# Seven products instead of eight on two blocks of every second channel, with block sums on GpSimd and VectorE

## The chip, the cores and the metric

The kernel runs on one core of a Trainium2 chip. Five engines matter here, each with its own instruction queue that it works through in order: TensorE (PE; its weight loads are shown as PEld), VectorE (DVE), ScalarE (ACT), GpSimd (POOL) and SyncE (SP), which here only issues transfers. TensorE writes its results to PSUM, eight banks of 512 float32 numbers per partition[...]. Everything else lies in SBUF, 128 partitions wide. All numbers are float32.

The metric is the device time of one execution in microseconds, lower being better. The kernel before took 3156.9 us (median of three runs, 3156.66 to 3157.14).

## The reference

Two layers follow each other on an input x of 384 x 384 positions with 128 channels. The first is a gated triangle product:

```python
z = layernorm(x)
left  = (z @ Wl + bl) * sigmoid(z @ Wlg + blg)
right = (z @ Wr + br) * sigmoid(z @ Wrg + brg)
core  = einsum('bikh,bjkh->bijh', left, right)      # 128 channels h, each 384 x 384 x 384
x1 = x + sigmoid(x @ Wg + bg) * (layernorm(core) @ Wout + bout)
```

The second is a row gate: x1 goes through a left, an equality, a right and a gate matrix, the right part is summed along each row, the product goes through an output matrix, and the result plus x1 is normalised. The change touches the line `core = einsum(...)` alone. For each of the 128 channels it is one matrix product of a 384 x 384 left half, transposed, with a 384 x 384 right half.

## The kernel before, in words

The kernel has three stages. The first (up to about 1000 us) normalises x, makes left and right, and stores them to memory as `lr_d`, ordered by channel; one corner of the data, the last two groups of 64 columns in the last of the three row blocks, stays in SBUF (`kept`). The second makes the core, channel by channel, and is the stage that is changed. The third (from about 1760 us) works row by row on the core, and ends with the output.

Every instruction is pinned behind the one that was written before it for the same engine (`seq`), so the order of each engine's queue is the order of the program text. Waits between engines are placed by the data: an instruction waits for what it reads, and for the readers of what it overwrites.

The core stage runs over h from 0 to 127. N is 384, P is 128, NB is 3. Per channel:

- Loading (`load_h`, L92): two transfers on SP bring left and right of channel h, interleaved element by element, into one of three buffers `lrh`. The transfer for channel h + 3 is written after the work on channel h, because it takes that channel's buffer.
- Filling (`fill`, L576 to L595): GpSimd copies the kept corner into place (`stay`, L584 to L587: four copies of 128 x 64, two into `lrh` for the left half and two into `rr` for the right half), and then pulls the right half out of the interleaved buffer into a contiguous one, `rr` (L592: two blocks, L593: the rest of the third). `rr` has two buffers. Channel h + 1 is filled while TensorE works on channel h.
- Multiplying (L610 to L614): nine products, row block by row block, each with a 128 x 128 block of the left half as weights and one 128 x 384 block of `rr` as moving operand. They accumulate in three PSUM banks, `pc`, of which there are two sets. A product of float32 is two instructions on TensorE.
- Draining (L620 to L627): ScalarE copies all three banks to `ct` (two buffers), then squares it into `sq` (one buffer). VectorE adds `ct` to the running sum `csum` (L622) and `sq` to the running sum of squares `csq` (L623). Both are 128 x 1152, and third-stage statistics come from them. SP stores `ct` to `core_d`, after the transfer for channel h + 3.

Channel 127 is treated apart: its first block is finished ahead, and the inverse deviation of that block is computed while the rest goes on (`variance`, `root`, `inverse`, `newton`, L527 to L559; buffers `ve`, `r` and `m` from a pool of their own).

Of the kernel before, what the change touches and what calls it, by code (L numbers as in the profile page):

```python
# [19 lines left out]
def triangle_then_gated_row_kernel(ctx: ExitStack, tc: tile.TileContext, a: dict, out: bass.AP):  # L20
# [31 lines left out]
    core_d = dpool.tile([N, H, N], F32, name="core_d")  # L52
# [3 lines left out]
    def seq(ins):  # L56

        return tc.keep_in_program_order(ins)
# [21 lines left out]
    with ExitStack() as ctx2:  # L80
# [16 lines left out]
        with tc.tile_pool(name="p1w", bufs=5, side="right") as wp, \  # L97
# [361 lines left out]
            for k, (n, q) in enumerate(steps):  # L459
# [54 lines left out]
                if k == len(steps) - 2 * G // 4 + 16:  # L514
                    assert not full
                    for h in range(2):
                        load_h(h)


        spool, rp = (end2.enter_context(tc.tile_pool(name=n, bufs=b, side="right", reuse_waits="tile"))  # L520
                     for n, b in (("stats", 1), ("rstd", 2)))
        roots = {}


# [1 line left out]

        def variance(b, s):  # L527
            if b not in roots:
                roots[b] = [rp.tile([P, N], F32, tag=n, name=n, bufs=c) for n, c in (("ve", NB), ("r", NB), ("m", 2))]
            ve, _, m = (w[:, s] for w in roots[b])  # L530
            if b > 0:
                seq(nc.scalar.activation(m, csum[:, b, s], AF.Square, scale=1.0 / H))
                seq(nc.scalar.activation(ve, csq[:, b, s], AF.Copy, scale=1.0 / H))
                seq(nc.gpsimd.tensor_tensor(ve, ve, m, ALU.subtract))
                seq(nc.gpsimd.tensor_scalar(ve, ve, 0.0, EPS, ALU.max, ALU.add))
                return
            seq(nc.vector.scalar_tensor_tensor(m, csum[:, b, s], 1.0 / (H * H), csum[:, b, s], ALU.mult, ALU.mult))
            seq(nc.vector.scalar_tensor_tensor(ve, csq[:, b, s], 1.0 / H, m, ALU.mult, ALU.subtract))
            seq(nc.vector.tensor_scalar(ve, ve, 0.0, EPS, ALU.max, ALU.add))

        def root(b, s=None):
            ve, r, _ = roots[b]
            seq(nc.scalar.activation(r, ve, AF.Sqrt))

        def inverse(b, s):
            _, r, m = (w[:, s] for w in roots[b])
            seq(nc.vector.reciprocal(m, r))  # L547

        def newton(b, s):
            ve, r, m = (w[:, s] for w in roots[b])  # L550
            if b > 0:
                seq(nc.scalar.activation(r, m, AF.Square))
                seq(nc.gpsimd.tensor_tensor(r, r, ve, ALU.mult))
                seq(nc.gpsimd.tensor_scalar(r, r, -0.5, 1.5, ALU.mult, ALU.add))
                seq(nc.gpsimd.tensor_tensor(r, r, m, ALU.mult))
                return
            seq(nc.vector.tensor_mul(r, m, m))
            seq(nc.vector.scalar_tensor_tensor(r, r, -0.5, ve, ALU.mult, ALU.mult))
            seq(nc.vector.scalar_tensor_tensor(r, r, 1.5, m, ALU.add, ALU.mult))  # L559

        with tc.tile_pool(name="p2r", bufs=2, side="right", reuse_waits="tile") as rrp, \
             tc.tile_pool(name="p2more", bufs=1, side="right", reuse_waits="tile") as more, \
             tc.tile_pool(name="p2out", bufs=2, side="right", reuse_waits="tile") as op, \
             tc.tile_pool(name="p2sq", bufs=1, side="right", reuse_waits="tile") as qp, \
             tc.tile_pool(name="p2ps", bufs=2, space=PSUM, reuse_waits="tile") as ps, \
             tc.tile_pool(name="p2one", bufs=1, space=PSUM, reuse_waits="tile") as ps1:
            csum = spool.tile([P, NB, N], F32, name="csum")
            csq = spool.tile([P, NB, N], F32, name="csq")
            seq(nc.vector.memset(csum, 0.0))
            seq(nc.vector.memset(csq, 0.0))  # L570

            inp.append(more)
            load_h(2)
            right = {}

            def fill(h):  # L576

                if h < H:
                    t = loaded2[h]
                    rr = right[h] = rrp.tile([P, NB, N], F32, tag="rr", name="rr")  # L580
                    i1 = G * (NG - KEEP)

                    def stay():
                        for (kb, ig), lrt in kept.items():  # L584
                            i = slice(ig * G, (ig + 1) * G)
                            seq(nc.gpsimd.tensor_copy(t[:, kb, i, 0], lrt[:, h, :, 0]))
                            seq(nc.gpsimd.tensor_copy(rr[:, kb, i], lrt[:, h, :, 1]))  # L587


                    if h > 0:  # L590
                        stay()
                    seq(nc.gpsimd.tensor_copy(rr[:, :NB - 1], t[:, :NB - 1, :, 1]))  # L592
                    seq(nc.gpsimd.tensor_copy(rr[:, NB - 1, :i1], t[:, NB - 1, :i1, 1]))  # L593
                    if h == 0:
                        stay()  # L595

            fill(0)
            for h in range(H):
                fill(h + 1)
                t, rr = loaded2.pop(h), right.pop(h)  # L600
                pc = ps.tile([P, NB, 512], F32, tag="pc", name="pc")
                banks = [pc[:, ib, :N] for ib in range(NB)]
                order = [(kb, ib) for kb in range(NB) for ib in range(NB)]
                if h == H - 1:


                    banks[0] = ps1.tile([P, 512], F32, name="pc0")[:, :N]
                    order.sort(key=lambda o: o[1] > 0)
                    seq(nc.scalar.activation(warm, mhalf[:, 0:1], AF.Sqrt, scale=-1.0))
                for kb, ib in order:  # L610
                    seq(nc.tensor.matmul(  # L611
                        banks[ib], lhsT=t[:, kb, ib * P:(ib + 1) * P, 0], rhs=rr[:, kb],
                        start=(kb == 0), stop=(kb == NB - 1),
                    ))  # L614

                ct = op.tile([P, NB, N], F32, tag="ct", name="ct")
                sq = qp.tile([P, NB, N], F32, tag="sq", name="sq")
                to = core_d[:, h, :].rearrange("(b p) j -> p b j", p=P)
                if h < H - 1:
                    seq(nc.scalar.copy(ct, pc[:, :, :N]))  # L620
                    seq(nc.scalar.activation(sq, ct, AF.Square))
                    seq(nc.vector.tensor_add(csum, csum, ct))  # L622
                    seq(nc.vector.tensor_add(csq, csq, sq))  # L623
                    load_h(h + 3)

                    queue = nc.sync if h < H - 3 else nc.scalar
                    seq(queue.dma_start(out=to, in_=ct))  # L627
                else:
                    seq(nc.scalar.copy(ct[:, 0], banks[0]))
                    seq(nc.scalar.activation(sq[:, 0], ct[:, 0], AF.Square))  # L630
                    seq(nc.scalar.dma_start(out=to[:16, 0], in_=ct[:16, 0]))
                    seq(nc.scalar.dma_start(out=to[16:, 0], in_=ct[16:, 0]))
                    seq(nc.vector.tensor_add(csum[:, 0], csum[:, 0], ct[:, 0]))
                    seq(nc.vector.tensor_add(csq[:, 0], csq[:, 0], sq[:, 0]))
                    seq(nc.scalar.copy(ct[:, 1:], pc[:, 1:, :N]))  # L635
                    variance(0, slice(0, N))
                    root(0)
                    inverse(0, slice(0, N))
                    newton(0, slice(0, N))
                    seq(nc.scalar.dma_start(out=to[:, 1:], in_=ct[:, 1:]))  # L640


                    seq(nc.gpsimd.dma_start(out=rstd_d[0:P, :], in_=roots[0][1]))
                    seq(nc.gpsimd.tensor_tensor(sq[:, 1:], ct[:, 1:], ct[:, 1:], ALU.mult))
                    seq(nc.gpsimd.tensor_tensor(csum[:, 1:], csum[:, 1:], ct[:, 1:], ALU.add))
                    seq(nc.gpsimd.tensor_tensor(csq[:, 1:], csq[:, 1:], sq[:, 1:], ALU.add))

# [333 lines left out]
```

## Time and profile before

| What | Value |
|---|---|
| median of the runs | 3156.9 us |
| the profiled execution's own time | 3154.78 us |
| its span in the profile | 3152.9 us |
| TensorE busy | 3135.5 us (99%) |
| VectorE busy | 2473.6 us (78%) |
| GpSimd busy | 2392.9 us (76%) |
| ScalarE busy | 1808.5 us (57%) |
| core stage, 1100 to 1740 us: DMA share and rate | 0.96, 283 GB/s |
| granted TensorE clock | 0.999 of full |

The profile records one execution. A group line names the code line, the engine, the operation, what it writes and reads with shapes, how often it ran, its total busy time and mean duration, and, after the last bar, how long the engine was idle just before such instructions and what released it. A tile's line gives the least, the median and the largest duration. A timeline line gives the start, the duration, and then the instruction. Matmuls are pipelined: a matmul's own duration is longer than the distance between two of them, so distances are read from starts. A busy GpSimd or VectorE instruction may in part be waiting inside.

### The profile page before, as it was taken

The page shows a single profiled execution, that of the slowest core. Times are in us where ns is not written, and L with a number is a line of the kernel's source. Part 1 is how long each engine was busy: PE and PEld are TensorE (multiplying, and loading weights), DVE is VectorE, ACT ScalarE, POOL GpSimd, SP SyncE. Part 2 cuts the span into 40 slices and gives each one's busy share as a digit, 9 for nine tenths or more (in the row PEclk, how much of TensorE's full clock was granted, in tenths as well). Part 3 has the DMA queues.
Part 4 walks back from the last instruction along what each step waited for, and adds up shares of the span by engine and source line. Part 5 has one row for each costly group of instructions (what it writes and reads, how often), then busy time and mean ns, then how long its engine had stood idle before and what let it go on. Part 6 is the DMA issues. An engine that isn't in the chain of part 4 may idle for free.

```text
span 3152.9 us, 44536 instructions
## 1 busy us (share of the span) xinstructions
PE 3135.5 (99%) x11306; PEld 2132.8 (68%) x11306; DVE 2473.6 (78%) x7409; ACT 1808.5 (57%) x3755; POOL 2392.9 (76%) x3066
## 2 busy tenths in 40 slices
PE   9999999999999999999999999999999999999998
PEld 4777777777776666666666666677777777777776
DVE  8888888888885555555555788888888888888998
ACT  4444444444444343343433577777777777777777
POOL 6888888888886656666566587788888888888887
PEclk9999999999999999999999999999999999999999
DMA  4978878788883999999999865666666666666562
GB/s 154 340 302 304 326 279 340 281 320 299 312 304 106 282 282 283 282 284 282 284 282 283 298 231 202 220 224 221 219 220 218 221 220 219 220 220 222 210 213 109
DMA packets 509102, 797.42 MB, mean 253 GB/s; under 512 B 56689, under 2 KB 419569, under 8 KB 492466
## 3 DMA queue, kind: packets, MB, share of 16 engines
q1 hardware_dynamic: 507552, 792.61, 74.0%
q8 instruction: 94, 1.54, 0.2%
q10 hardware_dynamic: 1234, 1.77, 0.2%
q14 instruction: 158, 1.29, 0.1%
q0 software_dynamic: 64, 0.20, 0.0%
HBM read 508.14 MB, written 286.36 MB: 252 GB/s over the span
## 4 chain that ended last, share of the span: by engine, by line
PE 98%; DVE 1%; ACT 0%; issue 0%; DMA 0%; POOL 0%; POOLq 0%; DVEq 0%; ACTq 0%
PE pr L372 31%; PE pc L611 23%; PE py L781 8%; PE pr L752 8%; PE pg L769 8%; PE pl L770 8%; PE pg L721 8%; PE py L782 4%; DMA core_d<-ct 0%; PE pt L335 0%; PE pq L729 0%; ACT py L816 0%; PE pb L740 0%; POOL rs L286 0%; DVE m L547 0%
## 5 line engine op out<-in xcount | busy, mean ns | idle before, releaser
L372 PE MATMUL pr<-wz,xc 128*128 128x512 f32 x2176 | 935.1, 592 | 0.0
L372 PEld LDWEIGHTS pr<-wz,xc 128*128 128x128 f32 x2176 | 670.5, 308 | 263.9 <-POOL xc L324 1.2
L383 ACT ACTIVATE sg<-pr,rs 128x256 f32<-128x256 f32 x1152 | 483.8, 471 | 508.3 <-ACT sg L383 354.7
L611 PE MATMUL pc<-rr,lrh 128*128 128x384 f32 x2304 | 743.3, 486 | 0.4 <-DVE lr L385 0.4
L611 PEld LDWEIGHTS pc<-rr,lrh 128*128 128x128 f32 x2304 | 452.0, 196 | 291.8 <-issue 1.1
L385 DVE SCALAR_TENSOR_TENSOR lr<-pr,rs,sg 128x256 f32<-128x256 f32 x1152 | 501.7, 477 | 164.3 <-ACT sg L383 158.9
L816 ACT ACTIVATE py<-py,nm,rs 128x128 f32<-128x128 f32 x1149 | 493.1, 430 | 159.7 <-DVE u L774 80.6
L781 PEld LDWEIGHTS py<-wo,u 128*128 128x128 f32 x2304 | 376.6, 191 | 97.5
L622 DVE TENSOR_TENSOR csum<-csum,ct 128x1152 f32<-128x1152 f32 x127 | 175.0, 1378 | 332.9 <-ACT ct L620 332.9
L781 PE MATMUL py<-wo,u 128*128 128x128 f32 x2304 | 402.1, 275 | 0.0
L620 ACT COPY ct<-pc 128x1152 f32<-128x1152 f32 x127 | 142.3, 1120 | 445.2 <-PE pc L611 439.7
L743 POOL TENSOR_TENSOR cs<-ct,rt 128x384 f32<-128x384 f32 x380 | 379.7, 1000 | 8.3 <-DMA rt<-rstd_d 4.4
L851 POOL TENSOR_TENSOR yt<-yt,lnb 128x384 f32<-128x384 f32 x380 | 380.6, 1003 | 2.9 <-DVE yt L845 2.6
L324 POOL TENSOR_TENSOR xc<-xc,bc 128x512 f32<-128x512 f32 x272 | 345.8, 1271 | 24.0
L286 POOL TENSOR_TENSOR rs<-nd,mhalf 128x8 f32<-128x8 f32 (+1 forms) x145 | 236.3, 1630 | 146.8 <-ACT sg L383 107.2
L796 DVE BATCH_NORM_STATS2 st<-py 128x6 f32<-128x128 f32 x1152 | 266.0, 286 | 87.2 <-PE py L782 85.1
L592 POOL COPY rr<-lrh 128x768 f32<-128x768 f32 x128 | 190.8, 1490 | 167.2 <-DMA lrh<-lr_d 156.4
L782 PE MATMUL py<-ident,x1T 128*128 128x128 f32 x1152 | 314.0, 273 | 0.0
L752 PE MATMUL pr<-cs,wc 128*128 128x384 f32 x768 | 313.5, 490 | 0.0
L769 PE MATMUL pg<-x1T,mat_L_conv_W_gate 128*128 128x384 f32 x768 | 310.7, 486 | 0.9 <-ACT g L772 0.9
L721 PE MATMUL pg<-xt,mat_L_conv_Wg 128*128 128x384 f32 x768 | 310.7, 487 | 0.3 <-ACT ct L635 0.2
L770 PE MATMUL pl<-x1T,mat_L_conv_W_left 128*128 128x384 f32 x768 | 310.5, 486 | 0.0
(124 smaller groups left out, 4302.2 us busy)
## 6 DMA issues: line engine op xcount, KB each, us to landing
lr_d<-lr SPq DMA_DIRECT2D x128, 1024.0 KB
lrh<-lr_d SPq DMA_DIRECT2D x128, 640.0 KB
xt<-in_x_row_dram SPq DMA_DIRECT2D x96, 768.0 KB
ct<-core_d SPq DMA_DIRECT2D x95, 768.0 KB
rt<-rstd_d SPq DMA_DIRECT2D x95, 768.0 KB
out_dram<-yt SPq DMA_DIRECT2D x94, 768.0 KB
core_d<-ct SPq DMA_DIRECT2D x125, 576.0 KB
xt<-in_x_nat_dram SPq DMA_DIRECT2D x136, 512.0 KB
```

The costliest lines, as they stand in the source:

```text
L372: seq(nc.tensor.matmul(pr[:, r, :], lhsT=columns[n][:, 4 * q + i, :] if n < PLAIN else columns[n][:, q, :, i], rhs=wz, start=True, stop=Tr ...
L383: seq(nc.scalar.activation(sg[r], pr[:, r, 2 * H:], AF.Sigmoid, scale=rs[r]))
L385: seq(nc.vector.scalar_tensor_tensor(t[:, :, c * XR + r0 + r, :], pr[:, r, :2 * H].rearrange("k (h s) -> k h s", s=2), rs[r], sg[r].rearra ...
L611: seq(nc.tensor.matmul(banks[ib], lhsT=t[:, kb, ib * P:(ib + 1) * P, 0], rhs=rr[:, kb], start=(kb == 0), stop=(kb == NB - 1),))
L721: seq(nc.tensor.matmul(pg[:, :N], lhsT=wg0, rhs=r["xT"], start=True, stop=True))
L752: seq(nc.tensor.matmul(pr[:, :N], lhsT=wc, rhs=r["cs"], start=True, stop=True))
L769: seq(nc.tensor.matmul(pg2[:, :N], lhsT=wgate, rhs=r["x1T"], start=True, stop=True))
L770: seq(nc.tensor.matmul(pl[:, :N], lhsT=wleft, rhs=r["x1T"], start=True, stop=True))
L781: seq(nc.tensor.matmul(py[:, s], lhsT=r["u"][:, s], rhs=r["wo"], start=True, stop=False))
L782: seq(nc.tensor.matmul(py[:, s], lhsT=r["x1T"][:, s], rhs=ident, start=False, stop=True, is_transpose=True))
L816: seq(nc.scalar.activation(py[:, s], py[:, s], AF.Identity, bias=bias, scale=scale))
L851: seq(engine.tensor_tensor(yt, yt, lnbb, ALU.add))
```

## The change

Even channels are multiplied as before, nine full products (`plain`). Odd channels from 1 to 125 are multiplied differently. Take the left blocks as A(k, i), row block k and column block i, and cut each right block of 384 columns into two halves of 192, B(k, j). For k, i and j in {0, 1} the sum of A(k, i) times B(k, j) over k is a 2 x 2 product of blocks, which takes eight half-width products in the plain way. Strassen's identity, in the form with few additions, does it with seven, on sums of blocks:

- left sums on GpSimd (`left_sums`, four sums of 128 x 128, into `ss`)
- right sums on GpSimd (`right_sums2`, one instruction for two sums and two more of 192 columns, into `tt`)
- sums of the products on VectorE (`add`, eight sums of 192 columns with one operand from PSUM), and one copy by ScalarE (`one`).

The third row block of k adds four half products, which accumulate into the same banks, and the third column block i stays three full products into `b4`. So an odd channel is 11 half-width and 3 full products, 17 half-widths where there were 18.

Around that the change moves work. The right half of an odd channel is pulled out by ScalarE (`apart`, three copies), not by GpSimd; the kept corner is still copied by GpSimd, now in the even channel's part, ahead of the left sums. `pc` has one set of three banks, because the odd channels take the other five. The even channel's banks are copied by ScalarE early in the odd channel; its squares and its sum follow there, and its sum of squares is added in the next even channel. The odd channel's third block is copied by ScalarE in the next even channel, and so are its square and both sums. Both stores wait accordingly. `ct` has three buffers; the buffers for the sums, `sq` and the inverse deviations share one allocation (`arena`). The last two channels are multiplied and drained as before.

```diff
-        spool, rp = (end2.enter_context(tc.tile_pool(name=n, bufs=b, side="right", reuse_waits="tile"))
-                     for n, b in (("stats", 1), ("rstd", 2)))
+        spool = end2.enter_context(tc.tile_pool(name="stats", bufs=1, side="right", reuse_waits="tile"))
+        arena = spool.tile([P, 2 + 2 * NB, N], F32, name="arena")
+        own_root = [[arena[:, n] for n in place] for place in ((0, 1, 2), (3, 5, 7), (4, 6, 2))]
...
-                roots[b] = [rp.tile([P, N], F32, tag=n, name=n, bufs=c) for n, c in (("ve", NB), ("r", NB), ("m", 2))]
+                roots[b] = own_root[b]
...
-             tc.tile_pool(name="p2out", bufs=2, side="right", reuse_waits="tile") as op, \
-             tc.tile_pool(name="p2sq", bufs=1, side="right", reuse_waits="tile") as qp, \
-             tc.tile_pool(name="p2ps", bufs=2, space=PSUM, reuse_waits="tile") as ps, \
-             tc.tile_pool(name="p2one", bufs=1, space=PSUM, reuse_waits="tile") as ps1:
+             tc.tile_pool(name="p2out", bufs=3, side="right", reuse_waits="tile") as op, \
+             tc.tile_pool(name="p2st", bufs=1, side="right", reuse_waits="tile") as stp:
...
+            J = N // 2
+            js = slice(0, J), slice(J, N)
+            one, base, more2, least = (arena[:, n, j] for n in (2, 2 * NB) for j in js)
+            tt = arena[:, 0:2].rearrange("p b n -> p (b n)").rearrange("p (q j) -> p q j", j=J)
+            ss = [arena[:, 2 * NB + 1, n * P:(n + 1) * P] for n in range(3)] + [stp.tile([P, P], F32, name="s4")]
+            sq = arena[:, NB:2 * NB]
...
+            def block(h, k, i):
+                return loaded2[h][:, k, i * P:(i + 1) * P, 0]
...
+            def stay(h):
+
+                t, rr = loaded2[h], right[h]
+                for (kb, ig), lrt in kept.items():
+                    i = slice(ig * G, (ig + 1) * G)
+                    seq(nc.gpsimd.tensor_copy(t[:, kb, i, 0], lrt[:, h, :, 0]))
+                    seq(nc.gpsimd.tensor_copy(rr[:, kb, i], lrt[:, h, :, 1]))
+
+            def left_sums(h):
+
+                for n, x, y, op in ((0, block(h, 0, 1), block(h, 0, 0), ALU.subtract),
+                                    (1, block(h, 0, 1), block(h, 1, 1), ALU.add),
+                                    (2, ss[1], block(h, 0, 0), ALU.subtract),
+                                    (3, block(h, 1, 0), ss[2], ALU.subtract)):
+                    seq(nc.gpsimd.tensor_tensor(ss[n], x, y, op))
+
+            def right_sums2(h):
+
+                rr = right[h]
+                seq(nc.gpsimd.tensor_tensor(
+                    tt[:, 0:2], rr[:, 0, js[1]].unsqueeze(1).to_broadcast([P, 2, J]),
+                    rr.rearrange("p b n -> p (b n)").rearrange("p (a m) -> p a m", a=2)[:, :, js[0]], ALU.subtract,
+                ))
+                seq(nc.gpsimd.tensor_tensor(tt[:, 2], rr[:, 0, js[0]], tt[:, 1], ALU.subtract))
+                seq(nc.gpsimd.tensor_tensor(tt[:, 3], rr[:, 1, js[0]], tt[:, 2], ALU.subtract))
+
+            def apart(h, k):
+
+                j = slice(0, N if k < NB - 1 else G * (NG - KEEP))
+                seq(nc.scalar.copy(right[h][:, k, j], loaded2[h][:, k, j, 1]))
+
+            def squares(h):
+                seq(nc.scalar.activation(sq, cts[h], AF.Square))
+
+            def add_sum(h):
+                seq(nc.vector.tensor_add(csum, csum, cts[h]))
+
+            def add_squares(h):
+                if h >= 0:
+                    seq(nc.vector.tensor_add(csq, csq, sq))
...
+            def add(out, ps, term):
+                seq(nc.vector.tensor_add(out, ps, term))
...
+                for h in range(H - 2):
+                    cts[h] = op.tile([P, NB, N], F32, tag="ct", name="ct")
+                    if h % 2 == 0:
+                        plain(h, [pc[:, i, :N] for i in range(NB)])
+                        add_squares(h - 2)
+                        right[h + 1] = rrp.tile([P, NB, N], F32, tag="rr", name="rr")
+                        stay(h + 1)
+                        left_sums(h + 1)
+                        if h > 0:
+                            seq(nc.scalar.copy(cts[h - 1][:, 2], b4))
+                            store_core(h - 1)
+                        for k in range(NB - 1):
+                            apart(h + 1, k)
+                        if h > 0:
+                            squares(h - 1)
+                            add_sum(h - 1)
+                            add_squares(h - 1)
+                        apart(h + 1, NB - 1)
+                        right_sums2(h + 1)
+                    else:
+                        rr, ct = right[h], cts[h]
+                        B = [[rr[:, k, j] for j in js] for k in range(NB)]
+                        product(b0, block(h, 0, 0), B[0][0])
+                        product(b1, ss[2], tt[:, 2])
+                        product(b2, ss[0], tt[:, 1])
+                        product(b3, ss[1], tt[:, 0])
+                        product(b4, block(h, 0, 2), rr[:, 0], True, False)
+                        seq(nc.scalar.copy(one, b0))
+                        seq(nc.scalar.copy(cts[h - 1], pc[:, :, :N]))
+                        store_core(h - 1)
+                        add(base, b1, one)
+                        add(more2, b2, base)
+                        add(base, b3, base)
+                        add(least, b2, base)
+                        product(b0, block(h, 1, 0), B[1][0], True, False)
+                        product(b0, block(h, 2, 0), B[2][0], False, True)
+                        product(b4, block(h, 1, 2), rr[:, 1], False, False)
+                        squares(h - 1)
+                        add_sum(h - 1)
+                        fill(h + 1)
+                        product(b1, ss[3], B[1][1], True, False)
+                        product(b1, block(h, 2, 0), B[2][1], False, True)
+                        product(b2, block(h, 2, 1), B[2][1])
+                        product(b3, block(h, 1, 1), tt[:, 3], True, False)
+                        product(b3, block(h, 2, 1), B[2][0], False, True)
+                        product(b4, block(h, 2, 2), rr[:, 2], False, True)
+                        add(ct[:, 0, js[0]], b0, one)
+                        add(ct[:, 0, js[1]], b1, base)
+                        add(ct[:, 1, js[1]], b2, least)
+                        add(ct[:, 1, js[0]], b3, more2)
+                    del right[h], loaded2[h]
                     load_h(h + 3)
...
+                    if h == H - 2:
+                        add_squares(h - 2)
+                        squares(h - 1)
+                        add_sum(h - 1)
+                        add_squares(h - 1)
+                        fill(h + 1)
```

More of the change, by code (lines that the diff above doesn't have):

```diff
@@ L595, in fill @@
                         stay()
-            fill(0)
[L598 to L623, printed above, removed]
-                    load_h(h + 3)
[L626 to L646, printed above, removed]
@@ new lines, in triangle_then_gated_row_kernel @@
+            J = N // 2
[4 more added lines that the diff above has]
+            sq = arena[:, NB:2 * NB]
+            cts = {}
+            def block(h, k, i):
+                return loaded2[h][:, k, i * P:(i + 1) * P, 0]
@@ new lines, in apart, with store_core @@
+            def apart(h, k):
[8 more added lines that the diff above has]
+                    seq(nc.vector.tensor_add(csq, csq, sq))
+            def store_core(h, queue=nc.sync):
+                seq(queue.dma_start(out=core_d[:, h, :].rearrange("(b p) j -> p b j", p=P), in_=cts[h]))
@@ new lines, in product, with plain @@
+            def product(to, lhsT, rhs, start=True, stop=True):
+                seq(nc.tensor.matmul(to, lhsT=lhsT, rhs=rhs, start=start, stop=stop))
+            def add(out, ps, term):
+                seq(nc.vector.tensor_add(out, ps, term))
+            def plain(h, banks):
+                for k in range(NB):
+                    for i in range(NB):
+                        product(banks[i], block(h, k, i), right[h][:, k], k == 0, k == NB - 1)
+            fill(0)
+            with tc.tile_pool(name="p2mix", bufs=1, space=PSUM, reuse_waits="tile") as mps:
+                pc = mps.tile([P, NB, 512], F32, name="pc")
+                b0, b1, b2, b3 = (mps.tile([P, 512], F32, name="b%d" % n)[:, :J] for n in range(4))
+                b4 = mps.tile([P, 512], F32, name="b4")[:, :N]
+                for h in range(H - 2):
[49 more added lines that the diff above has]
+                    del right[h], loaded2[h]
+                    load_h(h + 3)
+                seq(nc.scalar.copy(cts[h][:, 2], b4))
+                store_core(h)
@@ new lines, in triangle_then_gated_row_kernel @@
+            with tc.tile_pool(name="p2ps", bufs=2, space=PSUM, reuse_waits="tile") as ps, \
+                 tc.tile_pool(name="p2one", bufs=1, space=PSUM, reuse_waits="tile") as ps1:
+                for h in range(H - 2, H):
+                    t, rr = loaded2.pop(h), right.pop(h)
+                    pc = ps.tile([P, NB, 512], F32, tag="pc", name="pc")
+                    banks = [pc[:, ib, :N] for ib in range(NB)]
+                    order = [(kb, ib) for kb in range(NB) for ib in range(NB)]
+                    if h == H - 1:
+                        banks[0] = ps1.tile([P, 512], F32, name="pc0")[:, :N]
+                        order.sort(key=lambda o: o[1] > 0)
+                        seq(nc.scalar.activation(warm, mhalf[:, 0:1], AF.Sqrt, scale=-1.0))
+                    for kb, ib in order:
+                        seq(nc.tensor.matmul(
+                            banks[ib], lhsT=t[:, kb, ib * P:(ib + 1) * P, 0], rhs=rr[:, kb],
+                            start=(kb == 0), stop=(kb == NB - 1),
+                        ))
+                    if h == H - 2:
[4 more added lines that the diff above has]
+                        fill(h + 1)
+                    ct = op.tile([P, NB, N], F32, tag="ct", name="ct")
+                    to = core_d[:, h, :].rearrange("(b p) j -> p b j", p=P)
+                    if h < H - 1:
+                        seq(nc.scalar.copy(ct, pc[:, :, :N]))
+                        seq(nc.scalar.activation(sq, ct, AF.Square))
+                        seq(nc.vector.tensor_add(csum, csum, ct))
+                        seq(nc.vector.tensor_add(csq, csq, sq))
+                        seq(nc.scalar.dma_start(out=to, in_=ct))
+                    else:
+                        seq(nc.scalar.copy(ct[:, 0], banks[0]))
+                        seq(nc.scalar.activation(sq[:, 0], ct[:, 0], AF.Square))
+                        seq(nc.scalar.dma_start(out=to[:16, 0], in_=ct[:16, 0]))
+                        seq(nc.scalar.dma_start(out=to[16:, 0], in_=ct[16:, 0]))
+                        seq(nc.vector.tensor_add(csum[:, 0], csum[:, 0], ct[:, 0]))
+                        seq(nc.vector.tensor_add(csq[:, 0], csq[:, 0], sq[:, 0]))
+                        seq(nc.scalar.copy(ct[:, 1:], pc[:, 1:, :N]))
+                        variance(0, slice(0, N))
+                        root(0)
+                        inverse(0, slice(0, N))
+                        newton(0, slice(0, N))
+                        seq(nc.scalar.dma_start(out=to[:, 1:], in_=ct[:, 1:]))
+                        seq(nc.gpsimd.dma_start(out=rstd_d[0:P, :], in_=roots[0][1]))
+                        seq(nc.gpsimd.tensor_tensor(sq[:, 1:], ct[:, 1:], ct[:, 1:], ALU.mult))
+                        seq(nc.gpsimd.tensor_tensor(csum[:, 1:], csum[:, 1:], ct[:, 1:], ALU.add))
+                        seq(nc.gpsimd.tensor_tensor(csq[:, 1:], csq[:, 1:], sq[:, 1:], ALU.add))
```

## The prediction

> **What bounds the kernel now.** I read the page from the top: busy time, the slices, the chain, the costliest groups. The first line and the chain say that TensorE is never out of work, and that the core (L611) holds 23% of the time.
>
> ```profile
> PE 3135.5 (99%) x11306; PEld 2132.8 (68%) x11306; DVE 2473.6 (78%) x7409; ACT 1808.5 (57%) x3755; POOL 2392.9 (76%) x3066
> PE 98%; DVE 1%; ACT 0%; issue 0%; DMA 0%; POOL 0%; POOLq 0%; DVEq 0%; ACTq 0%
> ```
>
> Then the core stage alone, its groups and its busy time by stage (from 1100 to 1740 us): PE idle 0.0; DMA share 0.96; POOL 62% busy, but waiting 140.9/111 = 1.27 us per channel for the load.
>
> ```profile
> L611 PE MATMUL pc<-rr,lrh 128*128 128x384 f32 x1986 | 640.6, 486 | 0.0
> L592 POOL COPY rr<-lrh 128x768 f32<-128x768 f32 x111 | 168.2, 1515 | 140.9 <-DMA lrh<-lr_d 140.9
> 1100.00:1740.00 640.00, 640.00 (x1986) 389.31 (x1986) 351.36 (x221) 251.19 (x220) 396.97 (x662) 1.00 0.96 283
> ```
>
> The timeline of one channel gives the order in a period: the PSUM copy recurs every 5.81 us (1503.77, 1509.58). TensorE's new channel starts 0.2 us before that copy.
>
> ```profile
> 1503.77 1.12 ACT L620 COPY ct<-pc 128x1152 f32<-128x1152 f32 x1 [3.49 <-PE pc L611]
> 1503.87 0.24 POOL L587 COPY rr<-lr 128x64 f32<-128x64 f32 x1 [0.98 <-PE pc L611]
> 1504.93 1.36 DVE L622 TENSOR_TENSOR csum<-csum,ct 128x1152 f32<-128x1152 f32 x1 [2.49 <-ACT ct L620]
> 1505.26 1.77 POOL L592 COPY rr<-lrh 128x768 f32<-128x768 f32 x1 [0.79 <-DMA lrh<-lr_d]
> 1506.20 2.04 DVE L623 TENSOR_TENSOR csq<-csq,sq 128x1152 f32<-128x1152 f32 x1
> 1506.97 1.56 POOL L593 COPY rr<-lrh 128x256 f32<-128x256 f32 x1
> ```
>
> The last three lines matter most: L592, L623 and L593 run one after the other, not side by side. L592 starts under L622 and ends 0.74 us after it; L623 ends 1.21 us after L592; L593 ends 0.29 us after L623. The spreads (min/median/max ns) show what each costs alone and blocked:
>
> ```profile
> L592 POOL COPY rr<-lrh x52: 885/1611/2112, 1400.8 to 1696.7; 128x768 f32<-128x768 f32 x52
> L593 POOL COPY rr<-lrh x52: 403/1541/1621, 1402.5 to 1698.6; 128x256 f32<-128x256 f32 x52
> L623 DVE TENSOR_TENSOR csq<-csq,sq x52: 1349/2041/2079, 1401.7 to 1697.8; 128x1152 f32<-128x1152 f32 x52
> ```
>
> In the first stage a VectorE step of 16 elements behind a two-input GpSimd one ends as that ends (505.12 + 0.29 against 504.10 + 1.28); so GpSimd's sums hold VectorE off too.
>
> ```profile
> 504.10 1.28 POOL L324 TENSOR_TENSOR xc<-xc,bc 128x512 f32<-128x512 f32 x1
> 505.12 0.29 DVE L303 SCALAR_TENSOR_TENSOR nd<-nd,rs 128x16 f32<-128x16 f32 x1
> ```
>
> **What the Trainium skill says.** "SBUF — State Buffer", Who interferes with whom: a VectorE instruction with two SBUF inputs and a GpSimd one that reads SBUF exclude each other for a whole instruction, the first to start winning; with at most one SBUF input VectorE doesn't contend. The trace agrees (403 against 1541 ns). "GPSIMD Engine Reference", Elementwise — side-by-side cycle accounting: a two-input GpSimd step takes about 2.6 cycles per element; the rows below give 2.1 ns. "TensorE: Matmul & The Clock Gate", Wait — 56ns, not 53.3ns?: a warm matmul costs its columns plus 2.5 ns, so halving width costs little; the trace has 322.5 ns per instruction at 384 columns.
>
> **TensorE's part.** A channel is 9 products of two instructions: 18 x 322.5 = 5805 ns. Width 192 isn't shown. In the last stage three 128-wide instructions make a block, and blocks recur every 0.33 us, 110 ns each:
>
> ```profile
> 2500.24 0.38 PE L781 MATMUL py<-wo,u 128*128 128x128 f32 x2
> 2500.46 0.27 PE L782 MATMUL py<-ident,x1T 128*128 128x128 f32 x1
> 2500.57 0.39 PE L781 MATMUL py<-wo,u 128*128 128x128 f32 x2
> ```
>
> Between 110 and 322.5 the line gives 163 ns at 192 (161, half of 322.5, is the least; the weight load, 196 ns long, was hidden at 110 and is taken as hidden). An odd channel has 11 half and 3 full products: 22 x 163 + 6 x 322.5 = 5521 ns, 0.284 less. There are 63 (1 to 125): 17.9 us, if nothing holds TensorE.
>
> **What the other engines get.** Per pair of channels (11.33 us of TensorE, 11.61 before):
> - VectorE: four sums over 1152 (1.36 alone) and eight new adds over 192 from PSUM. 128x384 takes 559 ns, 1152 takes 1358, so 192 some 0.35: 5.4 + 2.8 = 8.2 us.
> - ScalarE: 0.32 (192 columns; 479 ns for 384), 1.12, 0.48, two squares of 1.16, three copies of the right half (0.52, 0.52, 0.42, priced by the 384-wide square, 523): 5.7 us.
> - GpSimd loses the big copies of odd channels (0.89 + 0.40) and gains seven sums. Prices:
>
> ```profile
> L534 POOL TENSOR_TENSOR ve<-ve,m x6: 455/456/459, 1814.1 to 1880.4; 128x128 f32<-128x128 f32 x6
> L743 POOL TENSOR_TENSOR cs<-ct,rt x380: 992/1000/1020, 1768.0 to 3129.3; 128x384 f32<-128x384 f32 x190
> ```
>
> So 2.125 ns per element and 0.18 fixed; 192 costs 0.59. Four left sums 1.82, right sums 1.0 + 2 x 0.59 = 2.18, eight small copies 1.9, the even channel's copies 1.29: 7.2 us. The left sums read every second word; L592 does so at 0.95 ns per element, so I add nothing (below is excluded, twice the price would add 1.1 us, all on the path).
> - DMA: same bytes; 0.96 of 5.805 is 5.57 us a channel, 11.15 a pair, inside 11.33. SP keeps each load at TensorE's end of a channel; stores move behind waits of about 2 us, but no load is behind an unfinished one for longer than that.
>
> No sum is above 11.33. But VectorE's 5.4 and GpSimd's 7.2 exclude each other: 12.6 in all (about 0.14 of each instruction is start-up outside the hold).
>
> **The path that decides.** GpSimd is in order. Its small copy into the next right half waits until TensorE has left the odd channel, and all seven sums stand behind it. The odd channel's second product needs the second right sum (tt 2), so it must be ready 5.805 + 0.33 = 6.13 us after the even channel starts. From that start:
> 1. VectorE's last Strassen add ends about -0.1 (last b3 product 0.65 before the end, result 0.17 later, add 0.35). The delayed squares add of the channel before follows and holds the port to 1.26.
> 2. GpSimd's first copy, ready at 0.30, ends at 1.35. VectorE's sum of the odd channel, waiting since 0.7, takes the port: 2.55.
> 3. Two more small copies: 2.8. The load has landed (0.9 + 1.27 = 2.2 on average). Left sums, two of them chained: 4.65.
> 4. First right sum 1.0, second 0.59, with 0.05 between: 6.3.
> 5. Somewhere in 3 or 4 VectorE's squares add intervenes (ScalarE: right copies from 2.2 to 3.25, square to 4.4): 1.0 to 1.2 more, 7.3.
>
> The second half product thus comes 1.2 us late. Net per pair 1.2 - 0.284 = +0.92; times 63 = +58 us. The profiled execution, 3154.8 us (span 3152.9 and 1.9 around it), becomes 3213; the median of the runs is 2.1 above it, so 3156.9 + 58 = **3215**.
>
> In the odd half all fits: GpSimd's third right sum and fill take about 3 us and a block of 1.2 within 5.5; base is needed 3.2 us after the odd start and comes at 1.3 or with tt 2; PSUM copies end 2 us in, before pc is written again. Behind the waiting second product stand all of TensorE's, so VectorE's adds, core stores and loads move with it; nothing else is late. The one-buffer pc, third ct and arena cost nothing then; without that cover (copy of pc not done by 5.5 us) the even channel would start late too, which needs 3.5 us more delay. The two tail channels are as before: their fill and sums have 5.8 us; I put them and the variance buffers at 0, between -2 and +3 us.
>
> **Rivals.**
> - TensorE stays the bound (faster): the holds fall in GpSimd's idle time. Without any hold the chain is 2.2 + 1.95 + 1.65 = 5.8, below 6.13. Then -17.9: 3139. For it: ScalarE could delay the squares add past tt 2. It decides from two holds fewer than my three; with one fewer the chain is 6.3, 0.17 late, and 63 x (0.17 - 0.284) = -7: 3150. Against it: VectorE's first two sums are ready by 0.7 us and the third by 4.4.
> - The holds and late landing add up: L592's longest wait was 3.1 us, so landing at 4.0, sums to 5.95, right sums 7.6, squares 8.7: 2.6 late if always. At half of that excess, 1.9: +102, 3259.
> - The DMA sets the pace: 11.15 us is close to 11.33. At 11.6 a pair nothing would be gained: 3157. Against: TensorE never waited for a load.
> - The identity saves no TensorE time since 192-wide instructions cost more than 163 ns: at 180 the odd channel gains nothing and stall alone stands, +75. Little speaks for it, as 128 wide runs at 110.
>
> **How the numbers follow.** Likeliest, three holds, 0.68: stall 0.8 to 1.5, 3189 to 3234. One or two holds fewer, 0.19: 3139 to 3170. DMA pace 0.03. Worse, 0.10: above 3234. For 8 in 10 the range runs from 3152 to 3245. About 0.2% is what can be told from no change: faster 0.18, same 0.05, slower 0.77.
>
> **What would show it.** Right: in the core TensorE waits about 1 us per odd channel, before the product that reads tt; the wait is for GpSimd; pairs take about 12.5 us; left and right sums show medians far above 456 and 592, or VectorE's sums above 1358. Half-width products spaced 163 ns confirm the price. Wrong: PE idle 0 in the core with pairs of 11.33, GpSimd done before the odd channel begins; or waits on DMA or VectorE instead.

## The result, and the profile after

The changed kernel takes 3236.6 us (median of four runs, 3235.8 to 3237.0), the kernel before 3157.0: a ratio of 1.025, 95% interval 1.023 to 1.027. It is 79.6 us slower. The forecast was 3215, its range 3152 to 3245.

The page of the changed kernel, busy time and then the chain by engine and by line, says what kind of loss it is:

```profile
PE 3134.5 (97%) x11936; PEld 2208.5 (68%) x11936; DVE 2575.4 (80%) x7913; ACT 1851.9 (57%) x4007; POOL 2615.6 (81%) x3381
PE 84%; POOL 14%; issue 1%; DVE 1%; ACT 0%; POOLq 0%; DVEq 0%; ACTq 0%
```

TensorE is no longer the whole chain: 14% of it is GpSimd's. Whose instructions these are, and who waits for them, stands in the waits of the core stage from 1100 to 1800 us (waiter, its line, whom it waited for; total, times, longest, in us):

```profile
...
POOL rr L613 <- PE b L652: 100.0, 55, 2.9
PEld b L652 <- POOL arena L630: 87.0, 54, 1.7
PE b L652 <- POOL arena L630: 71.3, 54, 1.4
...
ACT rr L636 <- DMA lrh<-lr_d: 3.0, 8, 0.9
```

L652 is TensorE's product, L630 the second right sum, L613 the kept corner's copy into the right half. TensorE waits for L630 once in each pair of channels, and hardly anything waits for a load. GpSimd itself stands idle for 100.0 us, 1.8 us a pair, before L613: the buffer that it fills is read by TensorE until the odd channel ends, and only then can the chain of sums start.

One even channel in the timeline of the changed kernel (start, duration, engine, line), with TensorE's lines and the three sums of VectorE beside GpSimd's queue:

```profile
1499.38 1.35 DVE L646 TENSOR_TENSOR csq<-csq,arena 128x1152 f32<-128x1152 f32 x1
1499.55 5.97 PE L652 MATMUL pc<-rr,lrh 128*128 128x384 f32 x18
...
1499.87 0.95 POOL L613 COPY rr<-lr 128x64 f32<-128x64 f32 x1 [1.76 <-PE b L652]
...
1500.64 1.39 DVE L642 TENSOR_TENSOR csum<-csum,ct 128x1152 f32<-128x1152 f32 x1
1500.77 1.39 POOL L612 COPY lrh<-lr 128x64 f32<-128x64 f32 x1
...
1502.11 0.23 POOL L613 COPY rr<-lr 128x64 f32<-128x64 f32 x1
1502.23 1.36 DVE L646 TENSOR_TENSOR csq<-csq,arena 128x1152 f32<-128x1152 f32 x1 [0.19 <-ACT arena L639]
1502.32 2.12 POOL L621 TENSOR_TENSOR arena<-lrh 128x128 f32<-128x128 f32 x2
1504.51 0.46 POOL L621 TENSOR_TENSOR arena<-arena,lrh 128x128 f32<-128x128 f32 x1
...
1505.04 0.46 POOL L621 TENSOR_TENSOR s<-lrh,arena 128x128 f32<-128x128 f32 x1
1505.35 0.49 PE L652 MATMUL b<-rr,lrh 128*128 128x192 f32 x2
1505.46 0.99 POOL L626 TENSOR_TENSOR arena<-rr 128x384 f32<-128x384 f32 x1
...
1506.53 0.59 POOL L630 TENSOR_TENSOR arena<-rr,arena 128x192 f32<-128x192 f32 x1
...
1507.18 1.24 PE L652 MATMUL b<-arena 128*128 128x192 f32 x6 [1.33 <-POOL arena L630]
```

Three times a sum of VectorE is under way when a GpSimd instruction starts, and each time the latter ends only after it: a copy of 64 columns takes 0.95 us, then one takes 1.39, then the first pair of left sums 2.12. Such a stretch, in which one of the two engines waits out the other's instruction, is a "hold"; "the port" is the prediction's word for what only one of the two can have at a time. The odd channel's first product starts at 1505.35, its second at 1507.18 where 1505.68 was due: 1.5 us late. The next even channel starts at 1512.47, so a pair takes 12.92 us against 11.61 before, 1.31 more.

The first odd channel, which has no earlier sums beside it, was only 0.2 us late. Between 1100 and 1700 us the mean pair takes 12.90 us, 1.29 more than before, so the other 62 cost about 80 us. The whole core stage, from the start of TensorE's first product to the start of its last, is 822.9 us long against 742.8 before, 80.1 more; the time from there to the end is 1400.3 against 1400.0.

### The profile page after: what moved, and what is told of

The parts are those of the page before. It is cut to its first block, busy times and chain, and to the rows that moved or that the text cites. A ratio compares the mean times of both kernels' runs of the same rounds, so it can differ in the third digit from the quotient of the medians.

```text
span 3233.9 us, 47068 instructions
## 1 busy us (share of the span) xinstructions
PE 3134.5 (97%) x11936; PEld 2208.5 (68%) x11936; DVE 2575.4 (80%) x7913; ACT 1851.9 (57%) x4007; POOL 2615.6 (81%) x3381
## 3 DMA queue, kind: packets, MB, share of 16 engines
q10 hardware_dynamic: 834, 1.18, 0.1%
## 4 chain that ended last, share of the span: by engine, by line
PE 84%; POOL 14%; issue 1%; DVE 1%; ACT 0%; POOLq 0%; DVEq 0%; ACTq 0%
PE pr L372 30%; PE b L652 11%; PE py L906 8%; PE pr L877 8%; PE pg L894 8%; PE pl L895 8%; PE pg L846 8%; POOL arena L621 5%; PE py L907 4%; POOL lrh L612 3%; POOL rr L613 2%; POOL arena L626 2%; POOL arena L630 1%; POOL s L621 1%; PE pc L652 0%
## 5 line engine op out<-in xcount | busy, mean ns | idle before, releaser
L652 PE MATMUL pc<-rr,lrh 128*128 128x384 f32 x1134 | 376.1, 486 | 0.4 <-DVE lr L385 0.4
L652 PEld LDWEIGHTS pc<-rr,lrh 128*128 128x128 f32 x1134 | 222.4, 196 | 144.0 <-issue 1.1
L655 DVE TENSOR_TENSOR arena<-b,arena 128x192 f32<-128x192 f32 x252 | 90.2, 358 | 274.3 <-PE b L652 258.7
L652 PE MATMUL b<-rr,lrh 128*128 128x192 f32 x1134 | 286.0, 379 | 0.0
L897 ACT ACTIVATE g<-pg,col_L_conv_b_gate 128x384 f32<-128x384 f32 x384 | 222.7, 580 | 104.4 <-PE pg L894 93.7
```

What stands on the lines that cost most here:

```text
L652: seq(nc.tensor.matmul(to, lhsT=lhsT, rhs=rhs, start=start, stop=stop))
```

## The experiments

All times are medians. The ratios are to the kernel before on the same chip: 3157.0 us beside the change, 3155.8 beside the others.

| Kernel | us | ratio to before, 95% interval | TensorE busy from 1100 to 1700 us, of 600 us |
|---|---|---|---|
| the change | 3236.6 | 1.0251 (1.0233 to 1.0269) | 538.8 |
| short sums | 3138.9 | 0.9947 (0.9932 to 0.9961) | 599.8 |
| squares early | 3187.6 | 1.0101 (1.0086 to 1.0116) | 574.1 |
| right sums on VectorE | 3139.2 | 0.9948 (0.9933 to 0.9963) | 599.4 |
| both moves | 3138.6 | 0.9946 (0.9930 to 0.9963) | 599.5 |
| no third hold | 3166.4 | 1.0032 (1.0020 to 1.0044) | 590.2 |
| one SBUF input | 3139.8 | 0.9948 (0.9931 to 0.9965) | 599.8 |

### VectorE's sums made short

```diff
-                seq(nc.vector.tensor_add(csum, csum, cts[h]))
+                seq(nc.vector.tensor_add(csum[:, :, :8], csum[:, :, :8], cts[h][:, :, :8]))
...
-                    seq(nc.vector.tensor_add(csq, csq, sq))
+                    seq(nc.vector.tensor_add(csq[:, :, :8], csq[:, :, :8], sq[:, :, :8]))
```

> The changed kernel with VectorE's running sums and squares of channels 0 to 125 over 8 of each 384 columns (24 elements instead of 1152); the statistics of the other columns are left out. Theory (VectorE's two-input sums hold the port that GpSimd needs): the three holds of some 1.2 us in the even channel vanish, GpSimd's 128x64 copies fall from 1348 ns to about 240 and the first left sums from 1049 to about 456, the second right sum is ready about 5 us after the even channel starts, TensorE has no wait, a pair takes 11.3 to 11.4 us, and the kernel 3137 to 3147 us. Rival (GpSimd's own work is too long): it stays within 10 us of 3236. Rival (the load comes too late once TensorE is faster): GpSimd waits for the load, and a pair takes 11.5 us or more.

It took 3138.9 us, and TensorE was busy 599.83 of 600 us. The groups of GpSimd from 1100 to 1700 us (count, total busy us, mean ns), first of the change and then of this kernel:

```profile
L612 POOL COPY lrh<-lr 128x64 f32<-128x64 f32 x93 | 126.0, 1354 | 0.0
L621 POOL TENSOR_TENSOR arena<-lrh 128x128 f32<-128x128 f32 x94 | 96.8, 1049 | 0.0
```

```profile
L621 POOL TENSOR_TENSOR arena<-lrh 128x128 f32<-128x128 f32 x106 | 54.6, 515 | 38.6 <-DMA lrh<-lr_d 38.3
L612 POOL COPY lrh<-lr 128x64 f32<-128x64 f32 x106 | 26.4, 249 | 0.1
```

GpSimd executes the same instructions, and the same copy falls from 1354 to 249 ns. The left sums fell to 515 ns, not to the 456 expected. In the channel that starts at 1499.49 the second right sum ends 5.4 us after TensorE's start, where 6.13 is the deadline. So its own work fits into the even channel; that rival is out. The load did come later, as the third theory said (38.3 us of waiting here in 106 sums), but it cost TensorE nothing. What this run leaves open is whether VectorE's second SBUF input counts, or its being busy as such.

### The port alone: the same sums with one SBUF input

The second operand of the even channel's three sums comes from a PSUM bank; `b0` is idle there.

```diff
+                def from_psum(to):
+                    to = to.rearrange("p b (t j) -> p (b t) j", j=J)
+                    seq(nc.vector.tensor_add(to, to, b0.unsqueeze(1).to_broadcast([P, 2 * NB, J])))
...
-                        add_squares(h - 2)
+                        if h > 0:
+                            from_psum(csq)
...
-                            add_sum(h - 1)
-                            add_squares(h - 1)
+                            from_psum(csum)
+                            from_psum(csq)
```

> The changed kernel with VectorE's three sums of the even channel kept at 1152 elements each, but with the second operand read from a PSUM bank of 192 columns, repeated six times, in place of from SBUF (what is summed is then not the core: that part of the statistics is left out). Port theory: VectorE is as busy as before in the even channel, but GpSimd isn't held up: small copies at 240 ns, left sums at 456 to 530 ns, TensorE doesn't wait, 3137 to 3150 us. Rival (VectorE's being busy, or the traffic as such, slows GpSimd): 3220 us or more.

It took 3139.8 us. The timeline of one even channel, VectorE and GpSimd:

```profile
1499.85 1.34 DVE L671 TENSOR_TENSOR csq<-csq,b 128x1152 f32<-128x1152 f32 x1
...
1500.52 0.24 POOL L612 COPY lrh<-lr 128x64 f32<-128x64 f32 x1
...
1500.70 0.24 POOL L613 COPY rr<-lr 128x64 f32<-128x64 f32 x1
1500.91 0.52 POOL L621 TENSOR_TENSOR arena<-lrh 128x128 f32<-128x128 f32 x1
1501.11 1.35 DVE L671 TENSOR_TENSOR csum<-csum,b 128x1152 f32<-128x1152 f32 x1
...
1502.37 1.35 DVE L671 TENSOR_TENSOR csq<-csq,b 128x1152 f32<-128x1152 f32 x1
1502.41 0.47 POOL L621 TENSOR_TENSOR arena<-arena,lrh 128x128 f32<-128x128 f32 x1
```

VectorE's sums are as long as before (1.34 to 1.35 us), and start at nearly the same places: 0.17 before TensorE's even channel (1500.02), then 1.09 and 2.35 us after it, where the change had 0.17 before, 1.09 and 2.68. Three of the GpSimd instructions shown lie wholly inside them at 0.24 to 0.47 us. So neither VectorE's being busy nor the SBUF traffic that is left (one operand read, one result written) slows GpSimd; the second SBUF input does. The even channel's running sum, which is made in the odd channel (L642), still reads two and still holds off the copies beside it; nothing urgent stands behind those.

### One hold taken away at a time

First the one that stands at the head of the even channel: the even channel's squares are added in the odd channel.

```diff
-                        add_squares(h - 2)
                         right[h + 1] = rrp.tile([P, NB, N], F32, tag="rr", name="rr")
...
                         squares(h - 1)
                         add_sum(h - 1)
+                        add_squares(h - 1)
                         fill(h + 1)
...
                     if h == H - 2:
-                        add_squares(h - 2)
                         squares(h - 1)
```

> The changed kernel with the even channel's squares added to their sum in the odd channel, right behind its sum, in place of at the start of the next even channel. Port theory: one hold of about 0.9 us leaves GpSimd's chain (its first small copy starts at 0.3 and isn't blocked), the other two stay: TensorE's wait falls from 1.5 to 0.6 to 0.9 us, 3182 to 3200 us. Rival (only GpSimd's own work counts): no change, 3236. Rival (VectorE's later adds of the odd channel come too late): slower than 3240.

It took 3187.6 us, 49 less than the change. Waits of this kernel, 1100 to 1700 us:

```profile
PEld b L652 <- POOL arena L630: 40.4, 50, 1.2
PE b L652 <- POOL arena L630: 26.0, 50, 0.9
```

From the start of the first product's second instruction to the start of the second product is 0.79 us in the median, where it was 1.66 in the change and is 0.163 without a wait. So 0.87 of the wait went with this hold, less than its 1.35 us, as it was under way before GpSimd's copy came; 0.63 stayed with the other two. In 18 of 50 channels GpSimd now waited for the load as well (14.1 us in all). The mean pair is 0.80 us shorter than the change's, and 62 x 0.80 = 50.

Then the last one:

```diff
                             add_sum(h - 1)
-                            add_squares(h - 1)
+                            seq(nc.vector.tensor_add(csq[:, :, :8], csq[:, :, :8], sq[:, :, :8]))
```

> The changed kernel with one of the three holds cut: the add of the odd channel's squares, last in VectorE's even channel, covers 8 of each 384 columns (the rest of those squares is left out). Port theory: GpSimd's chain is shorter by that hold, 1.2 to 1.25 us; TensorE's second odd product comes 0.2 to 0.4 us late in place of 1.5; 3236 - 62 x 1.2 = 3162, between 3150 and 3170 us. Rival (the holds overlap with other waits, so that one alone brings little): above 3190 us.

It took 3166.4 us, 70 less than the change, 1.13 per pair. TensorE still waits:

```profile
1510.49 0.49 PE L652 MATMUL b<-rr,lrh 128*128 128x192 f32 x2
1511.18 1.24 PE L652 MATMUL b<-arena 128*128 128x192 f32 x6 [0.20 <-POOL arena L630]
```

The second product is due at 1510.82 and comes at 1511.18, 0.36 late. So this hold, which came while GpSimd had work, was worth nearly its own length; with 0.36 of wait left, and 0.1 lost behind it (1511.18 to 1512.26 for six instructions, 0.98 without a wait), the gain of 0.28 is eaten: 62 x 0.18 = 11 us over the kernel before, as measured.

### The right sums on VectorE, and both moves

The sums stay two-input operations and go on excluding GpSimd and being held by it, but they leave GpSimd's queue, and they stand ahead of VectorE's sums of the odd channel.

```diff
             def right_sums2(h):
                 rr = right[h]
-                seq(nc.gpsimd.tensor_tensor(
+                seq(nc.vector.tensor_tensor(
                     tt[:, 0:2], rr[:, 0, js[1]].unsqueeze(1).to_broadcast([P, 2, J]),
...
-                seq(nc.gpsimd.tensor_tensor(tt[:, 2], rr[:, 0, js[0]], tt[:, 1], ALU.subtract))
-                seq(nc.gpsimd.tensor_tensor(tt[:, 3], rr[:, 1, js[0]], tt[:, 2], ALU.subtract))
+                seq(nc.vector.tensor_tensor(tt[:, 2], rr[:, 0, js[0]], tt[:, 1], ALU.subtract))
+                seq(nc.vector.tensor_tensor(tt[:, 3], rr[:, 1, js[0]], tt[:, 2], ALU.subtract))
...
                         for k in range(NB - 1):
                             apart(h + 1, k)
+                        right_sums2(h + 1)
...
                         apart(h + 1, NB - 1)
-                        right_sums2(h + 1)
```

> The changed kernel with the three right sums on VectorE, placed ahead of its sums of the odd channel, in place of on GpSimd behind the left sums. Port theory: GpSimd's chain ends with the left sums, before 6.1 us, VectorE has tt 2 at about 3 us, and TensorE doesn't wait or waits at most 0.2 us: 3138 to 3155 us. Rival (VectorE is full: 9.6 us of work a pair and the waits for the port): its first odd adds come over 2 us late and TensorE waits for them, 3160 us or more.

It took 3139.2 us: 16.6 us faster than the kernel before, and some 97 faster than the change. TensorE's timeline over a pair and the stage's busy times (PE, PEld, DVE, ACT, POOL, then clock, DMA share, GB/s):

```profile
1498.40 5.97 PE L652 MATMUL pc<-rr,lrh 128*128 128x384 f32 x18
1504.21 0.49 PE L652 MATMUL b<-rr,lrh 128*128 128x192 f32 x2
1504.53 1.14 PE L652 MATMUL b<-arena 128*128 128x192 f32 x6
1505.51 2.10 PE L652 MATMUL b<-rr,lrh 128*128 128x384 f32 x8
...
1509.72 2.74 PE L652 MATMUL pc<-rr,lrh 128*128 128x384 f32 x8
1100.00:1700.00 600.00, 599.36 (x2434) 437.72 (x2433) 505.77 (x796) 284.31 (x424) 423.86 (x740) 1.00 0.98 290
```

From 1498.40 to 1509.72 a pair is 11.32 us. Six half-width instructions take 0.98 us, 163 ns each. VectorE is 84% busy and GpSimd 71%, but neither is late: in the channel shown the second right sum ends at 1502.33, 3.9 us after TensorE's start (3 was expected, 6.13 is the deadline). The core stage is 725.6 us long against 742.8: 17.2 less.

Then the squares of the even channel are moved too:

```diff
-                        add_squares(h - 2)
                         right[h + 1] = rrp.tile([P, NB, N], F32, tag="rr", name="rr")
...
                         for k in range(NB - 1):
                             apart(h + 1, k)
+                        right_sums2(h + 1)
...
                         add_sum(h - 1)
+                        add_squares(h - 1)
                         fill(h + 1)
...
                     if h == H - 2:
-                        add_squares(h - 2)
                         squares(h - 1)
```

> Both moves: squares of the even channel added in the odd channel, and right sums on VectorE. Port theory: TensorE doesn't wait, 3137 to 3147 us. Rival (VectorE is full in the odd channel: four adds, two sums, four adds are 5.5 us): VectorE's last adds end about 2 us into the even channel, right sums only after 3.3 us, and the odd channel waits for tt 2 or for base: 3150 to 3180 us.

Both edits together (`right_sums2` on VectorE as above) took 3138.6 us, the same within its interval. Its rival did not come about, and there was nothing left for the first move to bring, since TensorE already had no wait.

## Why the prediction was right, and where it was off

**TensorE's part** held. The forecast was 5521 ns for an odd channel at 163 ns per half-width instruction; the spacing is 163 ns, and with no wait (right sums on VectorE) a pair takes 11.32 us (11.33 forecast). The whole gain was put at 17.9 us; the core stage of that kernel shows 17.2. Spacings of 110, 163 and 322.5 ns at 128, 192 and 384 columns come to 0.83 ns a column and about 4 ns fixed, so halving the width does cost little.

**The path that decides** was the one named: GpSimd's queue from the end of the odd channel to the second right sum. Its steps, in us after the even channel's start at 1499.55:

| Step | forecast | measured |
|---|---|---|
| 1: first hold ends | 1.26 | 1.18 |
| 2: first copy ends | 1.35 | 1.27 |
| 2: second hold ends | 2.55 | 2.48 |
| 3: small copies end | 2.8 | 2.79 |
| 5: third hold, where | about 4.4 | 2.68 |
| 3 to 5: second right sum ends | 7.3 | 7.57 |
| second odd product late by | 1.2 | 1.5 |

The third hold came elsewhere than forecast. ScalarE started to pull the right half out at 0.57 us, not at 2.2, and the loads had landed by then: ScalarE waited for them only 3.0 us in all from 1100 to 1800 us, against 50.9 from 1100 to 1700 us in the kernel with short sums, whose channels aren't slowed (DMA share 0.86 and 0.98). The place made no difference to the sum, as GpSimd had work at every point; "somewhere in 3 or 4" is all that the step needed.

**The size was off**: 58 us forecast, 79.6 measured, 0.92 against 1.31 us a pair. The terms that were too small belong to steps 3 and 5 and to what follows the wait. Step 5 said 1.0 to 1.2 for the third hold, and the sum took the lower end. The two left sums that read strided operands twice take 515 ns when nobody is beside them (short sums), not 456: 0.12 for both. The trace had their pair at 2.12 us, so against 0.98 undisturbed (two at 0.52, overlapping by 0.06) the hold was 1.14. These two, 0.14 and 0.12, are nearly all of the 0.27 by which the end of the chain was off. Then TensorE starts its product 0.06 after the sum has ended, and the six instructions after the wait take 1.08 us (1507.18 to 1508.26), not 0.98 as without a wait: together 0.16 that the forecast had at nothing. That leaves 0.39 - 0.43 = -0.04 for rounding, where the forecast's 1.17 became 1.2.

From the small copies on, the misses go the same way, so no lucky cancelling brought the forecast near. They carry the time just past the band of the case "three holds" (3189 to 3234), into "worse", which had 0.10, although three holds are what happened. Of the signs, the wait for GpSimd before the product that reads tt came (71.3 us in 54 channels, 1.3 each), and so did the spacing of 163 ns; pairs took 12.9 us, not 12.5. The medians of the sums did not rise as foretold: 518 ns for the first two left sums, of which one in each pair is held (the longest took 1693), and 589 for the second right sum. The holds sat in two small copies (0.95 and 1.39 us in the channel shown) and in that one left sum.

**The rivals.** "TensorE stays the bound" needed two holds fewer; with the holds of the even channel gone (short sums, one SBUF input) it is what happened, at 3139 to 3140, forecast 3139. With one hold fewer the forecast was 3150, and the two runs gave 3187.6 and 3166.4. Without the third hold the product came 0.36 us late where 0.17 was forecast: 0.12 of the difference is step 3 and 0.06 the start after the sum, and the 0.10 behind the wait comes on top. The first hold was worth less than the 1.0 us that the forecast took off: by steps 1 and 2 themselves only 0.8 (ready at 0.30, ended at 1.35, 0.24 long alone), and 0.87 as measured. The DMA didn't set the pace even where TensorE had no wait: 0.98 share and 290 GB/s, and pairs still took 11.32 us. "192 wide costs more" is ruled out by the spacing. Its sum was slightly off: 22 x 180 + 6 x 322.5 = 5895 ns is 0.09 us more than before, not nothing gained, so with the stall it should have read +81, which the measured total would have fitted.

The moves costed at nothing (one set of `pc`, the third `ct`, the shared allocation, later stores, the tail) stayed at nothing: TensorE's only wait inside the core's odd and even channels is for L630, and the time behind the core stage changed by 0.3 us.

That VectorE's sums with two SBUF inputs are what makes GpSimd late is shown by two runs: one only shortens them, the other keeps their length and place and takes away the second SBUF input. That the identity itself saves 17 us is shown by four kernels in which TensorE doesn't wait; two of them (right sums on VectorE, both moves) leave nothing out.

## What to carry to other kernels

Adding up each engine's work wasn't enough here: 8.2 us on VectorE and 7.2 on GpSimd (the forecast's sums) both fit into 11.3, yet in these runs the two excluded each other where VectorE read two operands from SBUF, so a chain on GpSimd has to be laid out with VectorE's holds in it. Before a gain on the bound engine is counted, follow the in-order queue that feeds it from its release to its deadline, and look for GpSimd instructions whose largest duration in the profile exceeds their least by nearly the length of a VectorE one (here 1397 against 231 ns, beside sums of 1.35 us): that excess is waiting, though it is shown as busy. The mend is to shorten the queue that has the deadline, even by giving work to the busier engine (VectorE at 84% here), or to give VectorE an operand from PSUM; the second was tried only with other values in the bank, so it shows the time and not yet a kernel. Not tried is a third buffer for the right half, with which GpSimd's small copies needn't wait until TensorE leaves the odd channel: it idles 1.8 us a pair there, and the second product was 1.5 us late.

## What the runs showed of the hardware that wasn't expected

- A small instruction can wait as long as a large one: a VectorE sum of 24 elements took 576 ns on average in the kernel with short sums, as it sat behind GpSimd's sums, while a GpSimd copy of 64 columns took 231 to 1397 ns in the changed kernel.
- A two-input GpSimd sum of 128 columns takes 515 to 520 ns with both inputs at every second word, about 460 with one of them contiguous, and 456 with both (L534 in the kernel before).
- After a wait of 1.5 us, six half-width instructions of TensorE took 1.08 us in place of 0.98; after a wait of 0.36 us (no third hold) they took 1.08 too (1511.18 to 1512.26). In the changed kernel's channel shown above the extra time lies between the first and the second of the six: 0.267 us where 0.162 is usual.
